# Layer 0's first tokens on Trainium2: each convolution tap in quadrants of its own, and the minimum's transpose behind the narrow conv steps

## The chip, the cores and the metric

The kernel runs on one NeuronCore of one Trainium2 chip. The metric is the device time of one execution in microseconds, as a median over runs. A profile of one execution gives every instruction's start, length and waits on five engines: TensorE (PE, with its weight loads PEld), VectorE (DVE), ScalarE (ACT), GpSimd (POOL) and SyncE (SP), which issues most transfers.

## The reference: what is computed

Two layers over a 64 x 64 image of 96 channels (4096 tokens). Each layer is a selective-scan mixer and an MLP with 8-bit rounding, both with a residual. What matters here is the front of layer 0's mixer:

```python
xz = x @ in_proj_w                       # 96 -> 2 * 192
x_val, z = xz[..., :192], xz[..., 192:]
xc = conv_general_dilated(xc, conv_w, (1, 1), 'SAME', feature_group_count=192) + conv_b   # 3 x 3, depthwise
x_val = silu(xc)
s1 = x_val, row by row;  s3 = x_val, column by column
y = scan(s1) + reversed scan(s1) + scan(s3) + reversed scan(s3)
decay = exp(cumsum(dt * A));  h = decay * cumsum(dB_u / (decay + 1e-12))
y = layernorm(y) * silu(z);  return y @ out_proj_w
```

The scan divides by decay + 1e-12. As the decay falls towards zero along the tokens, the states of all but the first tokens of a direction die out. The kernel uses this: it computes the scan only for the first 160 tokens (TE) of each of the four directions, and takes a second path over all tokens (`scan_all`) only if a minimum shows that some state has not died.

## The kernel before, in words

**The front of layer 0** (`front0`) normalizes the input by chunks of 512 tokens, transposes it, and multiplies by the input weights (`norm_in0`). The result lies in two padded images: `pad0` holds channels 0 to 127, with the upper and lower half of the image apart and the two channel halves turned round in the lower one; `pad1` holds the other 64 channels twice, once on partitions 0 to 63 and once on 64 to 127.

**The depthwise convolution** runs on TensorE: for each of the nine taps a 64 x 64 diagonal matrix (`self.diag`) multiplies a shifted view of the image, and the nine products of an output add up in PSUM. A 64 x 64 product uses one quadrant of the 128 x 128 array. Its row half is set by the partitions that it reads, its column half by the partitions that it writes (`LANES` are the two halves). There are two users of it.

`conv_ends` makes the first tokens of the four directions, into three PSUM tiles: t[0] and t[1] for channels 0 to 127, and t[2] for the other 64, with the forward way in its lower and the backward way in its upper partitions. It is called for o = 0 (by rows) and o = 1 (by columns), each in two turns, and each turn goes over all nine taps. For o = 0 a tap of a turn has one product into t[0], one into t[1] and one into t[2], of 192 columns each. For o = 1 it has two into t[0], two into t[1] (96 columns each) and one into t[2] (192). The t[2] product takes

```python
            at = (HW - n) * turn
            product(t[2][LANES[turn]], 1, LANES[1 - turn], (0, HW, at, n) if o else (at, n, 0, HW))
```

so that in turn 0 it reads the first three rows (or columns) of the image on partitions 64 to 127 and writes partitions 0 to 63, and in turn 1 the last three, the other way round.

`conv0` makes the whole convolution. It returns a list of steps: 18 wide ones (channels 0 to 127, four chunks, two turns of nine taps), nine narrow ones (the other channels), and the same again for the other chunks. `gate0` adds four steps for silu(z). These 58 steps are `beside`: `scan_ends` works on the first tokens on DVE and ACT, and `others(n)` puts the next n steps into the order of TensorE and ACT between its own instructions. All instructions passed to `keep` stay in program order on their engine.

**The order in `scan_ends`** is: `conv_ends` for o = 0 in both turns, `silu_ends(0)`, `conv_ends(1)` turn 0, `x_proj(0)` and `x_proj(1)`, `conv_ends(1)` turn 1, `silu_ends(1)`, `dt_proj(0)`, two wide steps, `x_proj(2)` and `(3)`, the broadcast loads `bce`, one wide step, `dt_proj(1)` and `(2)`, and then on DVE softplus polynomials, cumulative sums of dt and the products v. After the other 15 wide steps come the minimum over the last decays (`least`, `one`), the sigmoid and exponential on ACT, and the products on DVE. The minimum over partitions needs a transpose of the column `one`: a matmul into `leastt`, whose result DVE reads much later for `alive`. It stands ahead of the first narrow steps (the first `others(9)`).

`scaled(i)` multiplies half i of the conv's output by 4 D in place on ACT, once its stores `u` to memory have been read. `add_ends` then adds the first tokens' scan on DVE, from the tile x and from the PSUM tiles `yc`. At the end each engine reads `alive` and branches (L196); the program joins again in `back0`, whose first TensorE product is `m` (L1054).

The PSUM pool of the front, `pm`, has six buffers, which conv tiles, gate tiles z and yc share; the pool `pe` has two, for the small products, leastt among them.

Layer 0 ends with `back0` (norm, gate, output product and MLP), and layer 1 has a full convolution and a long scan over all tokens, which takes most of the time.

Of the kernel before, what the change touches and what calls it, by code (L numbers as in the profile page):

```python
# [40 lines left out]
HW = 64  # L41
# [47 lines left out]
LANES = (slice(0, 64), slice(64, 128))  # L89
# [21 lines left out]
class Net:  # L111
# [305 lines left out]
    def conv_ends(self, pm, ue, pad, o, turn):  # L417

        nc, keep = self.nc, self.keep
        n = TW // HW
        self.pad0_0, self.pad1_0 = pad
        if turn == 0:

            self.ends = [pm.tile([P, TW], F32, tag="m", name=f"ec{o}{k}") for k in range(3)]
        t = self.ends
        for tap in range(9):  # L430
            dy, dx = divmod(tap, 3)

            def product(t, g, r, at):
                at = (slice(at[0] + dy, at[0] + dy + at[1]), slice(at[2] + dx, at[2] + dx + at[3]))
                v = self.pad1_0[r, at[0], at[1]] if g == 1 else self.pad0_0[r, g // 2, at[0], at[1]]
                keep(nc.tensor.matmul(t, self.diag[g][r, tap], v, start=tap == 0, stop=tap == 8))


            for k, r in enumerate(LANES):
                way = (turn + k) % 2  # L440
                turned = LANES[1 - k]
                if o:
                    h = HW // 2
                    to = slice(h * n * way, h * n * (way + 1))
                    product(t[0][r, to], 0, r, (0, h, (HW - n) * way, n))
                    product(t[1][turned, to], 2, r, (0, h, (HW - n) * way, n))
                elif way:
                    product(t[1][turned], 2, r, (HW // 2 - n, n, 0, HW))
                else:
                    product(t[0][r], 0, r, (0, n, 0, HW))  # L450
            at = (HW - n) * turn
            product(t[2][LANES[turn]], 1, LANES[1 - turn], (0, HW, at, n) if o else (at, n, 0, HW))

    def silu_ends(self, ue, o):

# [128 lines left out]
    def scan_ends(self, ep, pm, ps, pad, beside):  # L584
# [7 lines left out]
        def others(n):  # L592
            for _ in range(n):
                next(beside)()

        def tile6(name, n=TE):
            return ep.tile([P, 6, n], F32, tag=name, name=name)
# [4 lines left out]
        o = 0  # L602
# [63 lines left out]
        for i, at in enumerate((XB, XC)):  # L666
            rows = self.dram.tile([4, TS], F32, tag=f"re{i}", name=f"re{i}")
            t = tile6(f"bce{i}", TS)
            o = 0
# [25 lines left out]
        buckets, o = [], 0  # L695
        for n0, n1, k in BUCKETS:
            buckets.append((n0, n1, n1 - n0, k, slice(o, o + (n1 - n0) * k)))
            o = buckets[-1][-1].stop
# [26 lines left out]
        keep(nc.vector.tensor_tensor(x, x, w, ALU.mult))  # L725
        keep(nc.vector.tensor_tensor(v, v, bc[1], ALU.mult))

        t = ps.tile([P, CH], F32, tag="e", name="leastt")
        keep(nc.tensor.matmul(t[0:1, 0:P], one, self.ident, start=True, stop=True))
        others(9)  # L730
        others(18)
        self.scaled(0)
        others(9 + 2)
        self.scaled(1)
        for s in range(6):
            keep(nc.vector.tensor_tensor_scan(x[:, s], keeps, x[:, s], 0.0, ALU.mult, ALU.add))
        for s in (slice(0, 3), slice(3, 6)):
# [307 lines left out]
    def keep(self, instruction):  # L1045
        self.tc.keep_in_program_order(instruction)
# [959 lines left out]
```

## Time and profile before

| | |
|---|---|
| median of 3 runs | 1513.44 us (1513.28 to 1515.28) |
| span of the profiled execution | 1503.4 us |
| busy PE / PEld | 1200.6 / 502.0 us |
| busy DVE / ACT / POOL | 1160.4 / 893.9 / 800.3 us |
| granted TensorE clock, mean | 0.829 |
| front, from the first conv_ends product to the first product after the branch | 37.82 to 132.40 us |

Busy time is the sum over an engine's instructions. A row of the timeline reads: start in us, length in us, engine, line, operation, output and inputs by tile name, shape, and how many instructions of that kind are merged in it; in brackets stand the idle time of the engine just ahead and what ended it. A float product shows as two records, since it runs in two passes. A row of the windows gives busy time and number of instructions of each engine in that stretch, then the clock that TensorE was granted (1.00 is full speed), the share of the transfer engines and GB/s. Line numbers are those of the listing above.

### The profile page before, as it was taken

To read this page: it belongs to the slowest core of one execution; us is meant where nothing else is said; L and a number is where in the kernel's file an instruction comes from. 1 tells how busy PE (TensorE), PEld (TensorE's weight loads), DVE (VectorE), ACT (ScalarE), POOL (GpSimd) and SP (SyncE) were. 2 spreads that over 40 slices of the span, in tenths; PEclk is the share of its full clock that TensorE was granted. 3 is DMA by queue.
4 is the path that set the end of the run, shared out by engine and by line. 5 is a ranking of instruction groups with operands and counts; after the bars stand their busy time and mean duration, and the time that the engine had idled before them with its cause. 6 is when DMAs were issued, how large, how long until landed. Compare 5 with 4: busy or idle time off the path is not lost. (4 is left out here: it accounts for less than half of the span.)

```text
span 1503.4 us, 12908 instructions
## 1 busy us (share of the span) xinstructions
PE 1200.6 (80%) x4020; PEld 502.0 (33%) x4020; DVE 1160.4 (77%) x849; ACT 893.9 (59%) x1062; POOL 800.3 (53%) x463
## 2 busy tenths in 40 slices
PE   7998887799996177777777877777776888899976
PEld 4623444342431022222222222222222433344344
DVE  6392445301507999999999999999999999999875
ACT  4345333302406777777777777777777777778435
POOL 1002221100202787778777777787778777775445
PEclk9998666799995588888889888888888898978855
DMA  2143000001406945454546353645374457442201
GB/s 63 32 141 80 1 11 16 17 14 35 140 23 187 274 135 183 160 179 137 188 133 217 114 190 122 231 117 188 117 237 145 157 177 249 124 139 86 86 1 43
DMA packets 66228, 183.73 MB, mean 122 GB/s; under 512 B 21425, under 2 KB 35397, under 8 KB 59333
## 3 DMA queue, kind: packets, MB, share of 16 engines
q1 hardware_dynamic: 64856, 182.53, 39.1%
q8 instruction: 34, 0.56, 0.1%
q10 hardware_dynamic: 1292, 0.28, 0.1%
q14 instruction: 46, 0.37, 0.1%
HBM read 155.98 MB, written 20.47 MB: 117 GB/s over the span
## 5 line engine op out<-in xcount | busy, mean ns | idle before, releaser
L1471 POOL TENSOR_TENSOR hss<-h1s,xws 128x1024 f32<-128x1024 f32 x96 | 224.5, 2373 | 138.3 <-PE hs L1479 134.1
L1455 ACT ACTIVATE da<-dt1s,a 128x1024 f32<-128x1024 f32 x168 | 188.0, 1119 | 148.1 <-DVE xws L1466 84.8
L1479 PE MATMUL hs<-hss,ident 128*128 128x512 f32 x376 | 216.2, 659 | 52.4 <-DMA x2s<-bc 33.3
L1466 DVE TENSOR_TENSOR_SCAN xws<-da,xws 128x1024 f32<-128x1024 f32 x96 | 224.2, 2335 | 8.3
L1455 ACT ACTIVATE da<-dt0s,a 128x1024 f32<-128x1024 f32 x168 | 187.4, 1116 | 72.4 <-DVE xws L1466 52.3
L1479 PE MATMUL hs<-h0s,ident 128*128 128x512 f32 x376 | 203.0, 623 | 0.5 <-DVE h0s L1466 0.5
L1466 DVE TENSOR_TENSOR_SCAN h1s<-da,h1s,xws 128x1024 f32<-128x1024 f32 x72 | 169.2, 2349 | 10.3 <-ACT da L1455 1.6
L1479 PEld LDWEIGHTS hs<-hss,ident 128*128 128x128 f32 x376 | 69.6, 203 | 188.2 <-issue 81.5
L1479 PEld LDWEIGHTS hs<-h0s,ident 128*128 128x128 f32 x376 | 75.8, 202 | 100.3 <-issue 94.7
L1500 PE MATMUL acc<-hc2s,fold 128*32 128x512 f32 x128 | 47.3, 828 | 61.0 <-POOL hc2s L1489 58.0
L1500 PE MATMUL acc<-hc0s,fold 128*32 128x512 f32 x128 | 47.5, 831 | 54.0 <-POOL hc0s L1489 54.0
L1311 POOL TENSOR_TENSOR du<-u,dt 128x1024 f32<-128x1024 f32 x6 | 14.6, 2441 | 135.6 <-DVE dt L885 129.4
L1500 PE MATMUL acc<-hc1s,fold 128*32 128x512 f32 x128 | 46.9, 822 | 49.9 <-POOL hc1s L1489 49.9
L1439 POOL TENSOR_TENSOR x2s<-x2s,dus 128x1024 f32<-128x1024 f32 x32 | 75.2, 2365 | 5.9 <-DMA x2s<-bc 5.9
L1466 DVE TENSOR_TENSOR_SCAN x0s<-da,x0s 128x1024 f32<-128x1024 f32 x32 | 74.7, 2335 | 4.3 <-ACT da L1455 2.0
L1466 DVE TENSOR_TENSOR_SCAN x1s<-da,x1s 128x1024 f32<-128x1024 f32 x32 | 74.7, 2335 | 3.7 <-ACT da L1455 1.2
L1466 DVE TENSOR_TENSOR_SCAN x2s<-da,x2s 128x1024 f32<-128x1024 f32 x32 | 74.7, 2335 | 3.6 <-ACT da L1455 1.1
L1439 POOL TENSOR_TENSOR x1s<-x1s,dus 128x1024 f32<-128x1024 f32 x32 | 75.0, 2358 | 0.1
L1479 PE MATMUL hs<-x0s,ident 128*128 128x512 f32 x128 | 68.0, 614 | 0.2 <-DVE x0s L1466 0.2
L1479 PE MATMUL hs<-x1s,ident 128*128 128x512 f32 x128 | 66.5, 601 | 0.0
L1439 POOL TENSOR_TENSOR x0s<-x0s,dus 128x1024 f32<-128x1024 f32 x28 | 65.8, 2361 | 0.0
L1183 PE MATMUL cv<-pad,cw 128*128 128x512 f32 x144 | 65.3, 609 | 0.0
(315 smaller groups left out, 2426.7 us busy)
## 6 DMA issues: line engine op xcount, KB each, us to landing
c0s<-bc SPq DMA_DIRECT2D x184, 128.0 KB, 2.7
c1s<-bc SPq DMA_DIRECT2D x184, 128.0 KB, 2.5
x2s<-bc SPq DMA_DIRECT2D x32, 512.0 KB, 6.0
x0s<-bc SPq DMA_DIRECT2D x28, 512.0 KB, 5.6
x1s<-bc SPq DMA_DIRECT2D x28, 512.0 KB, 6.6
dus<-du SPq DMA_DIRECT2D x20, 512.0 KB, 5.5
dt1s<-dt SPq DMA_DIRECT2D x40, 256.0 KB, 6.1
dt0s<-dt SPq DMA_DIRECT2D x40, 256.0 KB, 4.2
```

The lines of the kernel that those rows point to most:

```text
L1183: nc.tensor.matmul(t, cw[0][:, tap, 0:P], image(0, slice(0, P), n, tap), start=tap == 0, stop=False)
L1311: keep(nc.gpsimd.tensor_tensor(du, u[g][:, first * CH : first * CH + n], dt, ALU.mult))
L1439: keep(nc.gpsimd.tensor_tensor(x, x, du[:, part[j]], ALU.mult))
L1455: keep(nc.scalar.activation(das[i, s], dts[o][:, part[j]], AF.Exp, scale=self.a6[:, g, k : k + 1]))
L1466: keep(nc.vector.tensor_tensor_scan(to, da, x, start, ALU.mult, ALU.add))
L1471: keep(nc.gpsimd.tensor_tensor(cols(hs)[:, w, :], grid(h1)[:, w, :], grid(xw)[:, w, :], ALU.add))
L1479: keep(nc.tensor.matmul(t, self.ident, x[:, chunk(m)], start=x is hs, stop=x is xs[i % 3]))
L1500: keep(nc.tensor.matmul(to, self.fold4, src, start=k == 0, stop=k == NK - 1))
```

## The change

It has two parts.

First, the t[2] products of `conv_ends` move to other quadrants. For o = 0, turn 0 now makes the backward way of t[2] and turn 1 the forward way, so that the three products of a tap lie in three quadrants; before, t[2] lay in the quadrant of the t[1] product of the same turn. For o = 1, both ways are made in turn 0, each from the partitions that it writes to, so that they lie in two opposite quadrants; turn 1 has none. The number of products is the same, 36 for t[2] in all.

Second, the transpose into leastt moves behind the first nine narrow steps, so that TensorE need not wait for the minimum ahead of them. In the last part, `scaled(1)` moves ahead of the second gate step instead of behind it.

```diff
@@ -448,8 +448,11 @@
                     product(t[1][turned], 2, r, (HW // 2 - n, n, 0, HW))
                 else:
                     product(t[0][r], 0, r, (0, n, 0, HW))
-            at = (HW - n) * turn
-            product(t[2][LANES[turn]], 1, LANES[1 - turn], (0, HW, at, n) if o else (at, n, 0, HW))
+
+            for way in ((0, 1) if turn == 0 else ()) if o else (1 - turn,):
+                at = (HW - n) * way
+                r = LANES[way if o else 1 - way]
+                product(t[2][LANES[way]], 1, r, (0, HW, at, n) if o else (at, n, 0, HW))
 
     def silu_ends(self, ue, o):
 
@@ -725,13 +728,14 @@
         keep(nc.vector.tensor_tensor(x, x, w, ALU.mult))
         keep(nc.vector.tensor_tensor(v, v, bc[1], ALU.mult))
 
+        others(9)
         t = ps.tile([P, CH], F32, tag="e", name="leastt")
         keep(nc.tensor.matmul(t[0:1, 0:P], one, self.ident, start=True, stop=True))
-        others(9)
         others(18)
         self.scaled(0)
-        others(9 + 2)
+        others(9 + 1)
         self.scaled(1)
+        others(1)
         for s in range(6):
             keep(nc.vector.tensor_tensor_scan(x[:, s], keeps, x[:, s], 0.0, ALU.mult, ALU.add))
         for s in (slice(0, 3), slice(3, 6)):
```

## The prediction

> **What bounds the kernel now.** I read the page first, by slices of 37.6 us.
>
> ```profile
> PE   7998887799996177777777877777776888899976
> DVE  6392445301507999999999999999999999999875
> PEclk9998666799995588888889888888888898978855
> ```
>
> Both parts of the change lie in slices 2 to 4 (37 to 131 us), the front of layer 0. There PE is at 9, 9 and 8 tenths while DVE falls to 4: the front is a TensorE stage with other engines coupled to it, unlike the long scan after it, where DVE sits at 9. The timeline of TensorE in that stretch is the working view (start, duration, instruction, idle before it and who ended it):
>
> ```profile
> 37.82 16.36 PE L436 MATMUL ec<-pad,diag 64*64 64x192 f32 x198
> 54.11 0.50 PE L625 MATMUL xe<-ue,wx 128*80 128x160 f32 x2
> 55.82 5.52 PE L436 MATMUL ec<-pad,diag 64*64 64x96 f32 x90
> 61.27 0.80 PE L632 MATMUL de<-xe,w_dt 6*128 6x320 f32 x2
> 68.03 13.11 PE L516 MATMUL c<-pad,diag 64*64 64x512 f32 x120
> 84.11 0.59 PE L729 MATMUL leastt<-ident,least 128*1 128x128 f32 x2 [2.97 <-DVE least L720]
> 84.62 9.30 PE L535 MATMUL c<-pad,diag 64*64 64x512 f32 x72
> 93.76 15.62 PE L516 MATMUL c<-pad,diag 64*64 64x512 f32 x144
> 109.22 7.89 PE L535 MATMUL c<-pad,diag 64*64 64x512 f32 x72
> 117.04 1.98 PE L557 MATMUL z<-xt,w_in 96*128 96x512 f32 x4
> 132.40 3.78 PE L1054 MATMUL m<-y,mean 128*128 128x512 f32 x4 [3.13 <-ACTq L196]
> ```
>
> TensorE never stops from 37.82 to about 129.3 but for 2.97 us in front of leastt, and after the branch (L196) the rest of the program starts at 132.40. The reader is to see three things: the ec rows (23.45 us from 37.82 to 61.27 with their x_proj), the one gap, and that L535 takes 9.30 us behind the gap but 7.89 us the second time, x72 both times. The windows name the reason, columns being busy time and count for each engine, then the granted clock:
>
> ```profile
> core 0: us, PE busy (x) PEld busy (x) DVE busy (x) ACT busy (x) POOL busy (x), PEclk, DMA share, GB/s
> 81.10:84.10 3.00, 0.03 (x4) 0.02 (x1) 2.90 (x12) 2.90 (x5) 0.00 (x0) 0.98 0.87 227
> 84.10:93.80 9.70, 9.69 (x78) 3.16 (x82) 9.00 (x7) 9.64 (x5) 0.00 (x0) 0.83 0.77 235
> 93.80:117.00 23.20, 23.20 (x220) 7.32 (x212) 21.63 (x20) 7.01 (x9) 0.00 (x0) 1.00 0.22 70
> ```
>
> Last I read what the two other engines do at the ends of the front:
>
> ```profile
> 37.93 0.69 DVE L405 COPY pad<-in 128x512 f32<-128x512 f32 x1 [2.40 <-PE in L371]
> 83.80 0.16 DVE L720 TENSOR_REDUCE least<-least 128x1 f32<-128x7 f32 x1
> 125.52 1.73 DVE L768 TENSOR_TENSOR y<-y,bce 128x128 f32<-128x128 f32 x6 [9.85 <-ACT y L572]
> 123.49 3.03 ACT L572 ACTIVATE y<-y,d 128x2048 f32<-128x2048 f32 x2
> 129.32 0.60 ACT L562 ACTIVATE pad<-z 128x512 f32<-128x512 f32 x1 [0.36 <-PE z L560]
> ```
>
> ScalarE's last gate ends at 129.92 and is what the branch waits for. DVE waited 9.85 us for scaled(1) and was done at 128.80.
>
> **What the Trainium skill says.** "TensorE: Matmul & The Clock Gate", Part 3 (Packing small matmuls): matmuls in different row or column tiles of the array run side by side, a few ns apart. The trace agrees: L516 gives four quadrants a 512-column pass each, 144 passes in 15.62 us, so 36 rounds of 0.434 us. Part 1 of that page (The HAM clock gate) says that an idle window of about 3.4 us halves TensorE's clock; the trace has 2.97 us idle and then a granted 0.83 over the next stretch. The limit against concurrency is in "PSUM — Partial Sum Buffer", PSUM bank collisions: row tiles must not write one bank together, unless their column tiles, and so partitions, differ. The doubled t[2] products of o = 1 (rows 0-63 to partitions 0-63, rows 64-127 to 64-127) fit that; t[0] there is already written so.
>
> **Part 1, quadrants for o = 0.** Each product is two passes (108 records for 54). A 192-column pass costs 0.434 x 192/512 = 0.163 us. Before, t[2] shares the quadrant of t[1]: four passes in line, 0.65 us a tap, 18 taps 11.7 us, less some overlap where the turns meet. The trace shows about 11.2 (37.82 to 48.99). After, three quadrants hold two passes each, 0.326 us a tap, 18 taps 5.9 us. A new wait comes with it: turn 0 now takes the last rows of pad1 (way 1), which DVE copies at 37.93 to 38.62; in the compiled order that first t[2] product has a wait on DVE, and every later product is queued behind it. It starts at about 38.75 instead of 37.82: +0.9. So o = 0 costs 6.8.
>
> **Part 1, o = 1.** Here all four quadrants already work on 96 columns, and t[2] adds 192 to one of them: 2 x 288 columns a tap, 5.45 us over nine taps in turn 1, 0.606 a tap or 1.05 ns a column (strided reads, dearer than 0.85). After, turn 0 adds 192 to two opposite quadrants: same longest quadrant, 5.3 us. Turn 1 keeps 96 on each: 2 x 96 x 1.05 ns = 0.20 a tap, 1.8 us in all. Eight passes in 0.20 us is close together; the same page, Part 1, prices the least spacing at 25 ns, also 0.20, and the trace's densest like row is 90 passes in 5.52 us. I take 0.25 a tap, 2.2 us, with 1.8 and 2.7 as ends. x_proj (1.7 us) does not change: its silu then runs about 45 to 46.5 on an empty ScalarE, beside turn 0.
> Sum: 6.8 + 5.3 + 1.7 + 2.2 = 16.0 against 23.45, so 7.4 us (6.9 to 8.0). dt_proj, ScalarE's table load and softplus, the DVE polynomials and the bce loads all hang on it and move with it.
>
> **Part 2, leastt behind the narrow steps.** With the narrow conv first, TensorE goes on at 81.14 in old time instead of 84.11. Its two PSUM buffers are free: the pool has six and the wide steps hold four. `one` is ready 2.8 us after the wide steps end, narrow takes 7.9 us, so leastt does not wait any more; its reader is at 114.7. Saved: 2.97, and, as no idle window is left, the half clock behind it, 9.30 - 7.89 = 1.4 (0 if the clock falls for another reason). So 4.4 (3.0 to 4.4), all on TensorE's chain. DVE gains none of this. Together z starts 11.8 us earlier, at 105.2.
>
> **Part 3, scaled(1) behind the first gate.** It needs z0's three activations done and the u stores of the second narrow conv landed. z0 ends on ScalarE at about 108.9; those stores are issued 1 to 3 us behind their silu (105.4 to 106.6) and land a median 2.4 us after issue, by 110.7, when scaled's second half (after 1.99 us of the first) wants them: no wait, or some tenths. scaled ends at 112.0. What is queued behind it on ScalarE: z1 (112.0 to 113.8), z2, z3. z2's second tile needs z1's buffer, so TensorE pauses some tenths. DVE was ready at 115.67 - 7.4 = 108.3, waits some 3 us instead of 9.85, and ends its adds at about 114.2. In the compiled order z3's first and third tiles now wait for DVE (the yc buffers); these come free at 113.5 and 114.2, before TensorE reaches z3 at 114.8. Last gate: z3's product ends at about 117.8, ScalarE at 118.5, against 129.92. The end of the front moves by 11.4: Part 3 gives back 0.4.
>
> **After the branch** nothing in the code changes, and loads and scans start from the branch or what follows it. I carry the shift through: 1513.4 - 11.4 = 1502.0.
>
> **The rivals.**
> (B) The quadrants do not run side by side in these short products: then only leastt's part counts, less the new pad wait: 1513.4 - 4.4 + 0.9 = 1510. For it: 90 passes in 5.52 us is the shortest spacing yet seen here. Against: that row is as long as its one crowded quadrant explains, and L516 runs four at once.
> (C) DVE's chain, which gains only 7.4, sets the end: 1506. For it: it ran nearly without a break from 66 to 115. Against: its slack of 9.85 us ahead of the adds is more than the 4.4 it does not gain.
> (D) The earlier front pays more: no pad wait, turn 1 at 0.20, a better clock in what follows: 1513.4 - 13 to 15, about 1499.
> (E) Slower. From 132 to 289 us TensorE is busy 125 us at a granted 0.66, and the clock there comes and goes; the shift may place it worse. A mean of 0.59 would add 125 x (0.66/0.59 - 1) = 15 us, giving 1517. For it: the stage is uneven and TensorE-heavy. Against: the gap before the branch stays about 3 us, the work is the same, and the three times before lie within 2 us.
>
> **How the numbers follow.** Forecast 0.60, B 0.08, C 0.12, D 0.15, E 0.05. The range goes from 1497.5 (most of D) to 1507.5 (C): ends of Parts 1 and 2 give 1501 to 1504, the later clock a few us each way; B and E, and the far end of D, stay outside. Faster by over 0.2% (below 1510.4) is the forecast, C, D and half of B: 0.93; B's other half makes 0.03 for the same; 0.04 for slower.
>
> **What would show it.** In the changed profile: ec of o = 0 in about 6.8 us with a DVE wait near its start; turn 1 of o = 1 in 1.8 to 2.7; dt_proj at about 53.9; no idle time ahead of leastt; both narrow convs at 7.9 us; ScalarE's last gate at about 118.5 and the first mean product at about 121. Wrong if ec still takes 9 us or more, if z3 waits over a us for DVE, or if the stretch behind the branch differs in length by more than 3 us.

## The result, and the profile after

| | before | after |
|---|---|---|
| first comparison, median (4 runs each) | 1513.36 us (1511.59 to 1515.28) | 1495.87 us (1493.41 to 1499.89) |
| ratio, with its 95% interval | | 0.9887 (0.9861 to 0.9913) |
| span of the profiled execution | 1503.4 us | 1495.2 us |
| first ec product to the first product behind the branch | 94.58 us | 82.48 us |

The change makes the kernel faster. The first comparison puts it at 17.5 us, with 1495.87 us just under the predicted range; the two profiles show 12.1 us in the stretch that the change touches. Where the other 5 us come from is the question of the experiments. One number ahead of the prediction already pointed at it: the execution whose profile it reads took 1505.2 us (its span of 1503.4 and 1.8 more), 8 us less than the shortest of the three times given beside it.

The timeline of TensorE in the front, after the change:

```profile
37.86 0.54 PE L436 MATMUL ec<-pad,diag 64*64 64x192 f32 x4
38.80 11.08 PE L436 MATMUL ec<-pad,diag 64*64 64x192 f32 x212 [0.40 <-DVE pad L405]
49.81 0.50 PE L628 MATMUL xe<-ue,wx 128*80 128x160 f32 x2
51.52 2.06 PE L436 MATMUL ec<-pad,diag 64*64 64x96 f32 x72
53.51 0.80 PE L635 MATMUL de<-xe,w_dt 6*128 6x320 f32 x2
73.43 7.90 PE L538 MATMUL c<-pad,diag 64*64 64x512 f32 x72
81.26 0.38 PE L733 MATMUL leastt<-ident,least 128*1 128x128 f32 x2
97.07 7.91 PE L538 MATMUL c<-pad,diag 64*64 64x512 f32 x72
104.91 1.98 PE L560 MATMUL z<-xt,w_in 96*128 96x512 f32 x4
120.34 2.65 PE L1058 MATMUL m<-y,mean 128*128 128x512 f32 x4 [3.19 <-ACTq L196]
```

The first tokens' products reach x_proj at 49.81 instead of 54.11, and dt_proj at 53.51 instead of 61.27. Only 0.40 us of idle time is left on TensorE ahead of the branch, the new wait for pad1. leastt no longer waits, and both narrow convs take 7.9 us. ScalarE and DVE at the end of the front:

```profile
107.54 0.55 DVE L772 TENSOR_TENSOR y<-y,bce 128x160 f32<-128x160 f32 x2
110.53 1.73 DVE L772 TENSOR_TENSOR y<-y,bce 128x128 f32<-128x128 f32 x6 [2.44 <-ACT y L575]
112.29 1.52 DVE L772 TENSOR_TENSOR y<-y,yc 64x64 f32<-64x64 f32 x8
117.19 0.60 ACT L565 ACTIVATE pad<-z 128x512 f32<-128x512 f32 x1 [0.42 <-PE z L563]
```

DVE's wait for scaled(1) shrinks from 9.85 to 2.44 us, and the last gate still ends the front, at 117.79 instead of 129.92.

The windows of the program's five stretches, before and then after: the start, the front, `back0`, layer 1's conv and projections, and its scans with the tail. The columns are busy time and count by engine, then the granted clock of TensorE.

```profile
0.00:37.82 37.82, 28.23 (x109) 16.26 (x109) 25.06 (x56) 16.70 (x35) 6.80 (x43) 0.95 0.25 62
37.82:132.40 94.58, 88.48 (x783) 40.29 (x783) 55.98 (x100) 44.55 (x62) 0.00 (x0) 0.98 0.28 79
132.40:289.90 157.50, 126.06 (x400) 68.03 (x401) 74.64 (x171) 59.57 (x114) 35.35 (x48) 0.67 0.10 23
289.90:518.40 228.50, 185.65 (x651) 66.69 (x649) 91.05 (x65) 75.19 (x86) 43.05 (x18) 0.86 0.35 101
518.40:1503.40 985.00, 772.14 (x2080) 310.77 (x2080) 913.70 (x458) 697.86 (x767) 715.05 (x354) 0.83 0.47 149
```

```profile
0.00:37.86 37.86, 28.25 (x109) 16.26 (x109) 25.06 (x56) 16.70 (x35) 6.73 (x43) 0.95 0.26 62
37.86:120.34 82.48, 78.88 (x784) 35.27 (x783) 55.93 (x100) 44.55 (x62) 0.00 (x0) 1.00 0.32 91
120.34:279.40 159.06, 130.11 (x400) 69.25 (x401) 74.68 (x171) 59.45 (x114) 35.36 (x48) 0.65 0.10 23
279.40:511.30 231.90, 188.77 (x651) 67.47 (x649) 90.22 (x66) 75.73 (x87) 43.23 (x18) 0.84 0.35 99
511.30:1495.20 983.90, 765.27 (x2080) 309.75 (x2080) 913.84 (x457) 696.87 (x767) 714.84 (x354) 0.83 0.47 150
```

The front gains 12.1 us. In this pair the third and fourth stretches give back 1.6 and 3.4 us, each at a lower granted clock (0.65 for 0.67, 0.84 for 0.86) and with the same instructions. Behind the branch as a whole that makes 1371.0 and 1374.8 us, 3.8 us longer, where the prediction had called a difference of more than 3 us a sign of being wrong. So these two executions differ by 8.2 us, and the medians of the timed runs by 17.5: the rest of the program does not take the same time from run to run, and the prediction did not reckon with how much.

### The profile page after: what moved, and what is told of

Its sections match the earlier page's. It is cut to its first block, busy times and chain, and to the rows that moved or that the text cites. A ratio compares the mean times of both kernels' runs of the same rounds, so it can differ in the third digit from the quotient of the medians.

```text
span 1495.2 us, 12910 instructions
## 1 busy us (share of the span) xinstructions
PE 1191.3 (80%) x4020; PEld 498.0 (33%) x4020; DVE 1159.7 (78%) x849; ACT 893.3 (60%) x1062; POOL 800.2 (54%) x463
## 5 line engine op out<-in xcount | busy, mean ns | idle before, releaser
L1459 ACT ACTIVATE da<-dt1s,a 128x1024 f32<-128x1024 f32 x168 | 188.0, 1119 | 142.8 <-DVE xws L1470 82.6
L1504 PE MATMUL acc<-hc0s,fold 128*32 128x512 f32 x128 | 46.3, 812 | 54.4 <-POOL hc0s L1493 54.3
```

The source lines that it names most:

```text
L1459: keep(nc.scalar.activation(das[i, s], dts[o][:, part[j]], AF.Exp, scale=self.a6[:, g, k : k + 1]))
L1504: keep(nc.tensor.matmul(to, self.fold4, src, start=k == 0, stop=k == NK - 1))
```

## The experiments

Two theories of the excess, named F (only the front moves) and S (the rest gets shorter too, each time), were written down before the first four runs. A difference in us below is what the ratio makes of the median of the kernel before; the medians themselves can differ by some us more or less than that.

**The kernel before, as a control.** No edit.

> The kernel before, unchanged, as a control. Two theories of the 5 us by which the first comparison (1513.4 to 1495.9, 17.5 us) exceeds the 12.06 us that the profiles show at the branch. F (front only): the branch is reached at 132.4 us in every execution, and what follows has the same mean length in both kernels; its length varies by several us with the windows in which TensorE runs at half clock, mostly in layer 1's convolution, and four runs of each happened to fall 5 us apart. Then this profile's span minus its branch time differs from the first profile's 1371.0 us by some us, and the time is 1505 to 1515. S (systematic): the later part is longer by about 5 us whenever it starts at this point of time; then this profile's later part is near 1379, as the first timed runs were (1513.4, less about 1.8 between time and span, less 132.4).

Measured: 1511.83 us median of 22 runs, from 1502.69 to 1523.84; the kernel before beside it in 61 runs has 1511.65, from 1501.64 to 1523.72; ratio 1.0002 (0.998 to 1.0024). The front takes 94.7 us again. The profile's later part (from the branch on) is 1369.5 us, near the first profile's 1371.0 and 9.5 below S's figure; but it comes from an execution of 1504.88 us, one of the shortest of the 22, so alone it says little against S. One and the same kernel thus spreads over 22 us, where the four timed runs first seen lay within 4. Each run lists its mean granted clock: over the 22 runs of the control, time and clock have a correlation of -0.95, with 13.8 us less for each 0.01 more of clock.

**The changed kernel again, twice.** No edit.

> The changed kernel, unchanged. F: branch at 120.3, and the ratio to the kernel before drifts towards 1 - 12.1/1513 = 0.992 with more runs. S: the ratio stays at 0.9887, or 17 us.

> The changed kernel once more, for the ratio alone. F (only the front moves, by 12.1 us, and the rest is spread by TensorE's clock): the ratio to before lies near 0.992 again, and 17 us (0.9887) falls outside or to the edge of its interval; from the first to the last product of the front the profile has 82.5 us again, whatever the total. S (the rest is shorter by 5 us too): 0.9887.

Measured: 1497.99 us (8 runs), ratio 0.9915 (0.9881 to 0.995); and 1502.79 us (9 runs), ratio 0.9919 (0.9886 to 0.9952). Against 1511.65 and 1511.88 these are 12.8 and 12.2 us. The front is 82.6 and 82.8 us. The start differs, though: 44.4 and 46.3 us until the first ec product, for 37.9 in the first profile, so the branch came at 126.9 and 129.1 us and not at F's 120.3. In the ratio F holds: with more runs it went to the value that the front alone gives. S's 0.9887 lies at the lower edge of both intervals, so a small systematic rest isn't ruled out by these two alone. The profiles show none: behind the branch the changed kernel takes 1371 to 1375 us in three of them, and the kernel before 1371 and 1369 in two. F's place for the spread, mostly layer 1's convolution, does not hold: that stretch varies by 5 us over all profiles here, and the start by 10 over the nine that have the same code there.

**The quadrants alone.**

```diff
 (the kernel before)
-            at = (HW - n) * turn
-            product(t[2][LANES[turn]], 1, LANES[1 - turn], ...)
+            for way in ((0, 1) if turn == 0 else ()) if o else (1 - turn,):
+                ...
```

> The quadrants of t[2] alone; leastt and scaled(1) stand where they stood before. dt_proj(0) at 53.5 as in the changed kernel; TensorE again waits for the minimum, 2.8 to 3.0 us, ahead of the narrow conv, and if that idle stretch is what halves the clock, the first narrow conv takes 9.3 us again, and 7.9 if not. z starts at 109.3 (or 107.9), branch at 124.8 (123.4). F: 7.6 us faster than before; S: more than that by up to 5 us.

Measured: ratio 0.9946 (0.9924 to 0.9968), 8.2 us (4.8 to 11.5; the medians differ by 5.7). In the profile the front takes 86.99 us, 7.6 less than before. The wait is back, and the slow narrow conv behind it:

```profile
86.48 0.59 PE L731 MATMUL leastt<-ident,least 128*1 128x128 f32 x2 [2.97 <-DVE least L722]
87.00 9.16 PE L537 MATMUL c<-pad,diag 64*64 64x512 f32 x72
111.45 7.89 PE L537 MATMUL c<-pad,diag 64*64 64x512 f32 x72
```

This profile also has the longest start of all. The window of it:

```profile
0.00:47.77 47.77, 38.76 (x109) 21.45 (x109) 25.07 (x56) 16.71 (x35) 7.46 (x43) 0.71 0.19 49
```

109 product records as before, the same busy time on DVE and ScalarE, but a granted clock of 0.71 instead of 0.95, and 10 us more. The edit does nothing there.

**leastt and scaled(1) alone.**

```diff
 (the changed kernel)
-            for way in ((0, 1) if turn == 0 else ()) if o else (1 - turn,):
-                ...
+            at = (HW - n) * turn
+            product(t[2][LANES[turn]], 1, LANES[1 - turn], ...)
```

> leastt behind the narrow steps and scaled(1) ahead of the second gate, with the t[2] products in their old quadrants. dt_proj(0) at 61.3 as before; no idle time ahead of leastt, both narrow convs 7.9 us; z at 112.6, branch at 128.0. F: 4.4 us faster than before; S: the same part of the extra 5 us as of the shift, or none.

Measured: ratio 0.9954 (0.9934 to 0.9974), 7.0 us (3.9 to 10.0); F's 4.4 lies near the lower end. The front takes 90.08 us, 4.5 less than before, with no idle time ahead of leastt:

```profile
83.78 7.91 PE L536 MATMUL c<-pad,diag 64*64 64x512 f32 x72
91.61 0.38 PE L731 MATMUL leastt<-ident,least 128*1 128x128 f32 x2
107.43 7.90 PE L536 MATMUL c<-pad,diag 64*64 64x512 f32 x72
```

In the fronts the two parts add up: 7.6 + 4.5 = 12.1, which is what both together give.

**The changed kernel without the wait for pad1.** The turns of o = 0 change places, so that the last rows are wanted in the second turn.

```diff
-        for turn in range(2):
+        for turn in (1, 0):
             self.conv_ends(pm, ue, pad, 0, turn)
```

(and the tiles are made in the turn that now comes first)

> The changed kernel with turn 1 of o = 0 ahead of turn 0, so that the first t[2] product reads the first rows of pad1, which have long been there, and the last rows are wanted 3 us later. If the new wait for DVE costs what the timeline shows (38.80 less what would have been 38.07), ec to dt_proj takes 14.9 us instead of 15.6, the idle 0.40 is gone, and the branch comes 0.7 earlier: 81.8 us from the first ec product to the branch. Rival: another product has to wait for the same copy and the 0.7 us come back later in the stage (15.6).

Measured: one unbroken row in place of the two, and the front takes 81.67 us:

```profile
42.37 11.07 PE L436 MATMUL ec<-pad,diag 64*64 64x192 f32 x216
57.07 0.80 PE L635 MATMUL de<-xe,w_dt 6*128 6x320 f32 x2
```

From the first ec product to dt_proj it is 14.70 us instead of 15.65, so the wait cost 0.95, near the prediction's 0.9 and above the 0.7 expected for this run, and it does not come back. In the total (1499.73 us, ratio 0.991, 0.9874 to 0.9946) so small a step can't be seen.

**scaled(1) back behind the second gate.**

```diff
-        others(9 + 1)
+        others(9 + 2)
         self.scaled(1)
-        others(1)
```

> The changed kernel with scaled(1) behind the second gate again. The prediction says that the earlier place moves the last gate by 0.4 us to the later side and lets DVE end 3 us sooner. Then z to branch takes 15.0 here instead of 15.4. Rival: TensorE and ScalarE absorb either order, 15.4 in both, and only DVE's end moves.

Measured: from z to the product behind the branch 15.6 us, against 15.4 to 15.7 in the three profiles of the changed kernel and 15.4 and 15.5 before. DVE waits 5.30 us for scaled(1) instead of 2.44 and ends its adds 2.9 us later, without effect. The rival holds: the place of scaled(1) makes no difference here, and what the second part of the change gains is leastt's. The one time, 1494.38 us, says nothing next to the spread.

**The diagonals on GpSimd.** The starts of the profiles asked for an explanation. In the kernel before, DVE makes the three diagonals in the third round of the normalization, and TensorE waits for the round's xn (DVE, then TensorE):

```profile
12.72 1.42 DVE L274 TENSOR_TENSOR diag<-dup,cw 128x576 f32<-128x576 f32 x2
14.05 0.75 DVE L274 TENSOR_TENSOR diag<-dup,cw_turned 128x576 f32<-128x576 f32 x1
16.44 0.56 DVE L393 TENSOR_TENSOR lnxna<-lnxca,lnra 128x384 f32<-128x384 f32 x1
```

```profile
13.19 1.98 PE L371 MATMUL in<-xt,w_in 96*128 96x512 f32 x4 [0.67 <-ACT xt L409]
17.14 0.62 PE L397 MATMUL tr<-ident,lnxna 128*96 128x128 f32 x4 [1.98 <-DVE lnxna L393]
```

```diff
 (diagonals)
-                self.nc.vector.tensor_tensor(
+                self.nc.gpsimd.tensor_tensor(
```

It was run with the swapped turns three times, and alone on the kernel before. "The version before in this list" is the changed kernel with its turns swapped. The 2.8 us that its expectation names run from one weight load of TensorE to the next; between its products the wait is 1.98 us, as in the row above.

> The version before in this list, and the three diagonals (2.2 us on DVE in the third round of the normalization) made by GpSimd, which is idle there. Theory K: the run-to-run spread at the start (37.8 to 47.8 us until the first ec product in six profiles, with 3 to 27 us of half clock) begins with the stretch of 2.8 us in which TensorE waits while DVE makes the diagonals; without it the half clock doesn't set in, the start takes 33 to 36 us in every profile, and the mean is 4 to 6 us below the version before in this list. Rival: half clock sets in from elsewhere (the waits of each round); then the start is 2 us shorter on average and spread as before.

> The kernel before with the diagonals on GpSimd alone. Theory K: the start gets shorter and steadier by itself, independent of the change: 36 to 38 us to the first ec product with at most 7 us of half clock, where the nine profiles with the diagonals on DVE have 37.8 to 47.8 and a mean of 41.5; 94.6 us from there to the branch, as before; total 4 to 8 us under the kernel before. Rival (the gain of the earlier version came from the turns, or by chance): within 2 us of the kernel before.

> The version with swapped turns and diagonals on GpSimd again, to see whether its start stays short: K says 36 to 38 us and a ratio to before near 0.985; the rival says a start spread over 36 to 46 like the others, and a ratio nearer 0.990.

> The same once more, for its start alone: K 36 to 38 us, the rival anywhere from 36 to 46.

Measured, with the start (until the first ec product) and the half clock in it from each profile's clock record:

| kernel | start, us | half clock in it, us | ratio to before (95%) |
|---|---|---|---|
| nine profiles, diagonals on DVE | 37.8 to 47.8, mean 41.6 | 3 to 27 | |
| turns and diagonals, first | 37.2 | 7 | 0.9853 (0.9813 to 0.9893), 1491.87 us |
| the same, second | 35.7 | 0 | 0.985 (0.981 to 0.989), 1489.42 us |
| the same, third | 35.1 | 0 | one run, 1488.89 us |
| before, diagonals alone | 34.6 | 0 | 0.994 (0.9911 to 0.9968), 1501.95 us |

In the window of the second one, the start runs at full clock:

```profile
0.00:35.70 35.70, 27.78 (x111) 16.87 (x111) 24.82 (x53) 16.74 (x35) 10.58 (x46) 1.00 0.25 66
```

Three of the four starts have no half clock. The fourth has 7 us of it, from 11.5 on, ahead of where the diagonals stood, and its 37.2 us miss K's 33 to 36 (its median is 7.9 us under that of the swapped turns alone, where K had 4 to 6); the other three, of 34.6 to 35.7 us, are shorter than the 36 to 38 that K then expected. So K holds for most of the spread of the start, not for all.

The clock records say more. In the starts the clock changes only at the ends of windows of 3.41 us, and these windows lie differently in each profile. Half clock sets in in ten of the 13 starts, each time behind a window in which TensorE, counted from its product records, was busy for 23 to 55% of the time. In eight of the nine profiles with the diagonals on DVE that window ends at 16.8 to 19.8 us and holds 0.9 to 2.0 us of the wait for xn. In the ninth (the first repeat of the changed kernel) and in the start of 37.2 us it ends at 11.4 and 11.5 us, in the first rounds, so there half clock set in without that wait. In the three starts without half clock no window is below 64%.

The edit alone is worth 9.1 us (4.8 to 13.5) on the kernel before, where K had 4 to 8. Not all of it is clock: the edit also takes 2.2 us of work from DVE in that round. The version with the change, the swapped turns and the diagonals on GpSimd is 22 us under the kernel before. It was compared with the changed kernel only through that one.

The profile of the kernel before with the diagonals moved shows one thing more. It still has the wait for the minimum, of the same length, but not the slow conv:

```profile
80.88 0.38 PE L729 MATMUL leastt<-ident,least 128*1 128x128 f32 x2 [2.97 <-DVE least L720]
81.19 7.96 PE L535 MATMUL c<-pad,diag 64*64 64x512 f32 x72
```

Of four profiles with the 2.97 us of idle time, three have the half clock behind it and one has not. In the three, 2.5 to 2.8 us of the wait fall into one window of the clock record, in which TensorE is busy for 17 to 25%; in the fourth the wait is divided between two windows, at 66 and 47%. As windows of 48 to 55% had half clock behind them in the starts, that share is not the whole rule.

## Why the prediction was right and wrong

**The steps in the front were right, nearly to their numbers.** dt_proj was put at about 53.9 and came at 53.51; z at 105.2 and came at 104.91; the last gate at 118.5 and ended at 117.79; the first mean product at about 121 and came at 120.34. The front was to gain 11.4 us and gained 12.1. By its parts: the quadrants 7.4 forecast, 7.6 measured with leastt left in place; leastt 4.4 forecast, 4.5 measured with the quadrants left; the wait for pad1 0.9 forecast, 0.95 measured by taking it away. Inside the first part, o = 0 went from 10.8 us to 6.5 where 6.8 was forecast (the prediction's 11.2 for the old order is the end of a window that holds more than o = 0). Turn 0 of o = 1, with two full quadrants in place of one, took 5.45 us on both sides. Turn 1, whose fullest quadrant went from 288 columns a tap to 96, went from 5.45 us to 2.0; 2.2 was forecast. z3's wait for DVE and its pause for buffers, and with them the 0.4 that Part 3 was to give back, did not show: z to branch is 15.4 us on both sides.

**The rivals.** B, no concurrency, is out: with the turns swapped, 216 records of o = 0 and turn 0 follow each other in 11.07 us, where 198 took 16.36 before. C, DVE as the end, is out: DVE still waited 2.44 us and ended at 113.81, ahead of the last gate. D's total of about 1499 is close to what the later runs gave, but not for its reasons: the wait for pad1 was there, and the stretches behind the branch had the lower clock. E did not happen: the stretch behind the branch had 0.65 for 0.67 and 1.6 us more, not 0.59 and 15 us.

**What failed is the step "How the numbers follow": its term for the later clock, "a few us each way", and with it the width of the range.** Of the 17.5 us, 12.1 are the front, forecast at 11.4; the other 5.4 fall to the rest of the program, whose spread from run to run is the term that was too small. The prediction gave the later clock a few us, took the start for fixed, and leaned on three times that lay within 2 us, although the profile that it read came from an execution 8 us below them. (Its chances don't add up either: the forecast, C, D and half of B make 0.91, not 0.93.) The control shows 22 us between the runs of one kernel, and a correlation of -0.95 with the granted clock; the start alone has 10 us of that, `back0` and layer 1's conv some 3 to 5 each in the profiles here. Medians of four runs can then differ by several us from one set of runs to the next, and here they did: 17.5 us in the first comparison, 12.8 and 12.2 in the two with more runs. The centre, 11.4 us under before, lies inside both later intervals. The first four runs of the changed kernel had 0.8295 of the clock on average and a mean time of 1496.3 us, its 17 later runs 0.8256 and 1499.6. At the control's 13.8 us for each 0.01 that difference of the clock would be worth 5 us. So the runs support that the first four fell low by chance of the clock; which stretch was short in each of those four isn't known, as only one of them has a profile.

**Right for a partly wrong reason:** the half clock behind the 2.97 us wait. The prediction drew it from the wait and an idle window of about that length. It follows the wait in three of four profiles, and what differs in the fourth is how the wait lies in the windows of the clock. So the part counts for 1.3 to 1.4 us most of the time, not each time.

## What to carry to other kernels

When products of a tap or a head use quadrants of the array, write down for each turn which quadrant each product takes: in these turns the time went with the fullest quadrant, and moving one product of three was worth 4 us of 11 for o = 0 without any work removed. Put an instruction that waits for another engine behind work that is ready, and look what the new order wants first: the moved product brought a wait of its own, and swapping two turns removed it. Before a range is given, compare runs of the kernel over more than one sitting, and the granted clock of each: a profile of one execution can be exact to 0.3 us in a stretch (82.5 to 82.8 us for the front in three profiles of the changed kernel) and still say nothing about 10 us elsewhere. Also compare the profiled execution's own time with the times of the runs beside it.

## What the runs showed of the hardware that was not expected

TensorE's clock state differs between executions of one program, and a wait early on can cost more than its length. In the start of layer 0 of the kernel before, TensorE is busy 28 of 38 us. Where half clock sets in, at 11 to 20 us, it can stay for 24 to 27 us although TensorE is then busy most of the time (38.76 of 47.77 us), or end after 3.

The Trainium skill, "TensorE: Matmul & The Clock Gate", Part 1 (The HAM clock gate), says that about 3.4 us of sustained work bring full clock back and that the windows run freely. The traces agree: the lengths in these profiles are multiples of 3.4 us (3.4, 6.8, 10.2, 13.7, 23.9, 27.3), and in all ten starts with half clock the window ahead of the return was busy for 96 to 100%. What was not expected is how little keeps the half clock. Windows in which TensorE waited once for 0.67 us, and was busy for 80%, were never followed by full clock in these starts, for up to eight windows of half clock in a row, and some windows of 100% were not either. It was not expected either how little brings half clock on: the window ahead of it was not idle, but busy for 23 to 55% in these starts. These are counts over 13 profiles, and no run here changes the busy share of a window alone.
